# Graph attention on one core: the steps of the edge sums moved by one to three places in an eight-step order

## The chip, the cores and the metric

The program runs on one core of one Trainium2 chip. The metric is the device time of one execution in microseconds (us); lower is better. The core has a matrix engine (PE; its weight loads are shown apart as PEld), a vector engine (DVE), a scalar engine (ACT), GpSimd (POOL) and a queue engine that starts transfers (SP). Each works through its own list of instructions in the order in which the kernel was written out, and waits where an instruction needs another engine's result.

## What is computed

A graph of 12,500 nodes with 412,500 edges, sorted by target. Cut to what matters:

```
q, k, v, h = x @ Wq + bq, x @ Wk + bk, x @ Wv + bv, x @ Wn + bn
eh    = edge_features @ We + be
hmid  = leaky_relu(concat(q[src], k[tgt], eh) @ A1 + b1, 0.2)      # first layer, 128 wide
scores= leaky_relu(hmid @ A2 + b2, 0.2)                            # 8 heads
w     = softmax(scores.mean(-1), axis=0)                           # over all edges
out   = segment_sum(w[:, None] * v[tgt], src)                      # sums by source node
y     = layernorm(h + out) * gamma + beta
result= layernorm(x + y)
```

## The kernel before

Two streams of work are written into one order. The **edge stream** (`make`, lines 811 to 1081) takes the 403 groups of 1,024 edges in the given order. For each it multiplies one-hot matrices and edge features into "records" (`rows`, L940 and L947: the k and edge parts of the first layer beside v), evacuates them from the matrix engine's output banks (`evacuate`, L958 and L959, ACT) and scatters them by source block into a table `rtab` with POOL's indirect transfers (L970). Beside that DVE builds one-hots (L860 to L880) and the places of the records (L910 to L923), with counts on PE (L889). A group has six pieces.

The **sum stream** (`sums_of`, from line 1118) reads the records back by blocks of source nodes. There are 250 units of up to 16 tiles of 128 records, in ten rounds of 25. A unit goes through these functions:

- `load` starts the transfer of its records into `rt` (L1154, SP); `sources`, `turned`, `put` and `spread` bring the source numbers into `rowB`; `load_q` fetches `qs`.
- four times, for four tiles each: `onehot` (L1232, DVE), `hidden` (L1244 and L1254, PE: the first-layer rows), `copied` (L1265, ACT: out of the bank), `leaky` (L1269, DVE).
- once: `scores` (L1280, PE), `above` (function `above_zero`, L1294, ACT: the tile z), `heads` (L1306, PE), `maxima` (L1316 and L1321, DVE), `maximum` (L1327, PE), `reference` (L1336 and L1337, DVE), `weights` (L1346, ACT).
- four times: `select` (L1355, DVE, tile ohs), `weigh` (L1369, ACT, tile ohw), `add` (L1402, PE, into the bank psm).
- once: `lowered` (L1388 and L1391, ACT), `before_it` (L1379, SP: the table `old`), `total` (L1419, in the first rounds L1412, DVE: psm into old), `store` (L1431, SP).

The sum stream's order is a table of numbers, `lags` (line 1109): each function has a step, counted from the unit's own step s0, and a unit begins every 8 steps. So all functions of successive units share a frame of 8 steps. Within a step the older unit's work stands first; a few calls (`copied`, `leaky`, `maximum`) are put at the end of their step. While edge groups are left, the steps are spread evenly between the pieces of the edge groups, some 1.1 to 1.6 pieces to a step; what is left of the steps then runs alone, and a closing part normalizes the 98 blocks of nodes.

Buffers that bear on the order: psm is one bank (in the last round a second one is there, and units alternate), psS one, the ring of banks for rows, hidden and scores has five, ohs two, ohw three, hm six, rt six (eight in the last round).

Of the kernel before, what the change touches and what calls it, by code (L numbers as in the profile page):

```python
# [478 lines left out]
def sorted_path(  # L479
# [266 lines left out]
    above = const.tile([P, P], BF)  # L746
# [362 lines left out]
    def lags(p):  # L1109

        return dict(
            every=EVERY, lead=25 if p == NR - 1 else 19, sources=-13, turned=-12, spread=-7, q=-7,
            onehot=-2, copied=2, leaky=4, scores=12, above=14, heads=15, maxima=17, maximum=18,
            reference=20, weights=21, old=16, lowered=24, select=19, weigh=21,
            add=(24, 25, 27, 28), total=30, store=33,
        )

    def sums_of(bp):


        plans, s0, free, starts, ends = [], 19, ([], []), {}, {}
        for p, bs, t in units:
            nt = len(bs) * t
            nk = -(-nt // 4)
            o = lags(p)
            if plans:
                s0 += plans[-1][4]["every"]


            mine = free[spare_buffer(len(plans))]  # L1130
            held = MORE if mine is free[1] else BLKS
            load_at = mine[-held] + 1 if len(mine) >= held else 0
            s0 = max(s0, load_at + o["lead"] - 1)
            if plans:
                s0 = max(s0, plans[-1][2] + EVERY)
            if plans:
                s0 += (plans[0][2] - s0) % EVERY
            load_at = max(load_at, s0 - o["lead"])
            mine.append(s0 + o["add"][-1])
            starts.setdefault(p, load_at)  # L1140
            ends[p] = load_at
            plans.append((nt, nk, s0, load_at, o))
        steps = {}

        def do(step, fn, *args, late=0):
            steps.setdefault(max(int(step // 1), 0), []).append((late + step % 1, fn, args))
# [288 lines left out]
        def pieces(i):  # L1435
            at = list(range(0, plans[i][0], 4)) + [plans[i][0]]
            return list(zip(at[:-1], at[1:]))

        for i, (nt, nk, s0, load_at, o) in enumerate(plans):
            do(load_at, load, i)  # L1440
            do(s0 + o["sources"], sources, i)
            do(s0 + o["turned"], turned, i)
            do(s0 + o["turned"], put, i)
            do(s0 + o["spread"], spread, i)
            do(s0 + o["q"], load_q, i)
            for k, (c, c1) in enumerate(pieces(i)):
                n, s = c1 - c, s0 + 2 * k
                t = units[i][2]
                for u in range(-(-c // t), (c1 - 1) // t + 1):
                    do(s + o["onehot"], onehot, i, u)  # L1450
                do(s, hidden, i, c, c, n, k)
                do(s + o["copied"], copied, i, c, c, n, k, late=1)
                do(s + o["leaky"], leaky, i, c, c, n, k, late=1)
            do(s0 + o["scores"], scores, i, 0, nt)
            do(s0 + o["above"], above_zero, i)
            do(s0 + o["heads"], heads, i, 0, nt)
            do(s0 + o["maxima"], maxima, i)
            do(s0 + o["maximum"], maximum, i, late=1)
            do(s0 + o["reference"], reference, i)
            do(s0 + o["weights"], weights, i)  # L1460
            do(s0 + o["old"], before_it, i)
            do(s0 + o["lowered"], lowered, i)
            for j, t0 in enumerate(range(0, nt, 4)):
                n = min(4, nt - t0)
                if t0 % SEL == 0:
                    m = min(SEL, nt - t0)
                    do(s0 + o["select"] + 2 * j, select, i, t0, m)
                do(s0 + o["weigh"] + 2 * j, weigh, i, t0, n)
                do(s0 + o["add"][j], add, i, t0, n)
            do(s0 + o["total"], total, i)  # L1470
            do(s0 + o["store"], store, i)
# [350 lines left out]
    with tc.manual_schedule():  # L1822
# [9 lines left out]
        for i, _ in enumerate(_ for p in range(NP) for _ in make(p)):  # L1832
            while fills and fills[-1][0] <= i:
                fill_piece(*fills.pop()[1])
            while made < nt and made * n0 < i * nt:
                next(tabs, None)
                made += 1
            while sent < ne and sent * n0 < i * ne:
                next(more, None)
                sent += 1  # L1840
            if i == n1:
                for _ in tabs:
                    pass
                for _ in more:
                    pass
                spans()
                covered()
                tab_pool.close()
                steps, starts = sums_of(pool("blk", BLKS))
            if i < n1:  # L1850
                continue
            while r + 1 < NR and i >= 6 * begun[r + 1]:
                r += 1
            if r + 1 < NR:
                until = starts[r] + (starts[r + 1] - starts[r]) * (i - 6 * begun[r]) / (
                    6 * (begun[r + 1] - begun[r])
                )
                while done < until:
                    for fn, args in steps[done]:
                        fn(*args)  # L1860
                    done += 1
# [86 lines left out]
```

## Time and profile before

| what | value |
| --- | --- |
| runs shown | 5669.4, 5674.84, 5681.69 us; median 5674.84 us |
| the profiled execution's own time | 5666.23 us |
| its span from the first to the last instruction | 5664.4 us |
| mean granted PE clock over it | 0.831 |

The profile is of one execution. A group's row reads: line, engine, operation, the tile written and those read, shapes, how often; behind the bar the busy time in us and the mean of one in ns; behind the next bar the time that the engine sat idle just before such instructions, and what ended it. A row of waits gives who waited for whom, the total in us, how often, and the longest. A table of stretches gives for each stretch its length, then each engine's busy time (with the number of instructions), the granted PE clock as a share of full speed, the busy share of the transfer engines and the rate in GB/s. The ends of matrix instructions are modelled, so their busy time is approximate.

### The profile page before, as it was taken

The numbers are of one execution on the slowest core, as the hardware profiler recorded it, in microseconds if no ns is written. First come the engines' busy times: TensorE is split into PE (matmuls) and PEld (weight loads), VectorE is DVE, ScalarE is ACT, GpSimd is POOL, SyncE is SP. The second block draws the span as 40 slices with busy tenths as digits, with TensorE's granted clock in tenths as the row PEclk, the third lists the DMA queues.
The fourth block names the chain that finished last, engine by engine and source line by source line (L and its number), as shares of the span: only waits on it lengthen the run. The fifth ranks groups of instructions, "written<-read, shape, count | busy, mean of one in ns | idle before, by whom it ended". The sixth has DMA issues, their size and how long they took to land. (4 is left out here: it accounts for less than half of the span.)

```text
span 5664.4 us, 91119 instructions
## 1 busy us (share of the span) xinstructions
PE 4379.9 (77%) x29928; PEld 3200.3 (56%) x29928; DVE 3987.4 (70%) x8452; ACT 3097.1 (55%) x8846; POOL 3431.3 (61%) x3279
## 2 busy tenths in 40 slices
PE   4555536777788888888888888888887888887997
PEld 2333324555565666555566665666665565655777
DVE  7777736666667777766677767777776776766787
ACT  2432214444555666555566666666665665655786
POOL 4777666666666655566666666665556666666113
PEclk6666657788888889888888888888888998888999
DMA  6888756677788888877788878887887887878985
GB/s 194 264 260 263 250 197 223 224 240 229 247 267 272 268 268 278 261 263 257 268 269 279 294 264 282 284 278 263 275 266 270 280 285 265 271 262 274 345 314 188
DMA packets 727116, 1487.05 MB, mean 263 GB/s; under 512 B 157377, under 2 KB 326356, under 8 KB 724839
## 3 DMA queue, kind: packets, MB, share of 16 engines
q1 hardware_dynamic: 535538, 1055.66, 57.4%
q0 software_dynamic: 154752, 424.43, 20.6%
q10 hardware_dynamic: 36340, 1.05, 0.4%
q8 instruction: 237, 3.88, 0.3%
q14 instruction: 249, 2.03, 0.1%
HBM read 901.45 MB, written 579.32 MB: 261 GB/s over the span
## 5 line engine op out<-in xcount | busy, mean ns | idle before, releaser
L970 POOL DMA_INDIRECT rtab<-rec,idx x3224 | 3346.1, 1038 | 1896.5 <-issue 846.7
L958 ACT ACTIVATE rec<-bank 128x512 f32<-128x512 f32 x1612 | 881.0, 594 | 1265.8 <-remote 482.9
L1402 PE MATMUL psm<-rt,ohw 128*128 128x128 f32 x7448 | 1227.5, 310 | 158.3 <-issue 146.3
L1369 ACT ACTIVATE ohw<-ohs,w 128x128 f32<-128x128 bf16 x3724 | 1216.6, 403 | 37.3 <-DVE ohs L1355 24.1
L1402 PEld LDWEIGHTS psm<-rt,ohw 128*128 128x128 f32 x7448 | 1069.7, 216 | 243.5 <-issue 198.6
L1265 ACT ACTIVATE hm<-bank 128x512 f32<-128x512 f32 x932 | 550.0, 590 | 605.9 <-PE psm L1402 146.3
L947 PE MATMUL bank<-WeS,eat 64*128 64x128 f32 x6448 | 730.2, 333 | 109.2 <-issue 105.9
L940 PE MATMUL bank<-kvs,ohd 128*128 128x256 bf16 x3224 | 589.5, 303 | 259.8 <-ACT rec L958 116.9
L910 DVE TENSOR_TENSOR ats<-pc,oh 128x792 f32<-128x792 f32 x403 | 393.6, 977 | 560.4 <-remote 202.8
L1244 PE MATMUL bank<-ident,rt 128*128 128x128 f32 x3724 | 670.4, 303 | 68.9 <-issue 64.2
L947 PEld LDWEIGHTS bank<-WeS,eat 64*128 64x128 f32 x6448 | 530.6, 215 | 337.1 <-issue 331.9
L1232 DVE TENSOR_SCALAR ohT<-rowB,iotaP,power 128x512 bf16<-128x512 uint8 (+1 forms) x980 | 569.2, 584 | 160.2 <-remote 57.0
L1254 PE MATMUL bank<-ohT,qs 128*128 128x512 bf16 (+3 forms) x2156 | 628.5, 385 | 48.1 <-issue 39.3
L1244 PEld LDWEIGHTS bank<-ident,rt 128*128 128x128 f32 x3724 | 473.2, 155 | 334.0 <-issue 227.8
L1269 DVE SCALAR_TENSOR_TENSOR hm<-hm 128x512 f32<-128x512 f32 x932 | 637.5, 684 | 9.5 <-ACT hm L1265 6.8
L880 DVE TENSOR_SCALAR ohd<-dstb,node 128x1152 bf16<-128x1152 uint8 x404 | 566.1, 1401 | 40.0 <-remote 31.3
L940 PEld LDWEIGHTS <-ohd 128*128 128x128 bf16 x3224 | 335.1, 110 | 442.0 <-issue 345.5
L1306 PE MATMUL psS<-headsum,z 128*128 128x4 f32 (+2 forms) x2000 | 304.4, 274 | 165.2 <-ACT z L1294 155.6
L1306 PEld LDWEIGHTS psS<-headsum,z 128*128 128x128 f32 (+2 forms) x2000 | 297.8, 224 | 224.3 <-ACT z L1294 199.4
L1355 DVE TENSOR_TENSOR ohs<-iotaE,sl 128x512 bf16<-128x512 bf16 x932 | 394.0, 423 | 36.5 <-ACT ohw L1369 32.8
L1280 PE MATMUL bank<-hm,A2s 128*32 128x512 f32 x1864 | 377.7, 664 | 42.7 <-issue 32.7
L921 DVE TENSOR_REDUCE pos<-ats 128x8 f32<-128x792 f32 x403 | 390.3, 968 | 2.6
(199 smaller groups left out, 3683.9 us busy)
## 6 DMA issues: line engine op xcount, KB each, us to landing
rt<-rtab SPq DMA_DIRECT2D x192, 2056.0 KB
eat<-in_ea SPq DMA_DIRECT2D x201, 512.0 KB
rt<-rtab SPq DMA_DIRECT2D x48, 1542.0 KB
qs<-qtab SPq DMA_DIRECT2D x240, 256.0 KB
atab<-old SPq DMA_DIRECT2D x240, 256.0 KB
old<-atab SPq DMA_DIRECT2D x216, 256.0 KB
rtab<-rec,idx POOLq DMA_INDIRECT x3224
dstb<-dtab SPq DMA_DIRECT2D x201, 256.0 KB
```

Of the source, the lines that this page charges most:

```text
L880: nc.vector.tensor_scalar(to, row[:, cols], node, None, op0=ALU.is_equal)
L940: nc.tensor.matmul(pk[h][:, i, :], ohd[h * (GT // 2) + j + i], kvs, start=(i == 0), stop=False,)
L947: nc.tensor.matmul(pk[h][:, i, :D], eat[half, (j + i) * P : (j + i + 1) * P], WeS[half, :], start=False, stop=(i == 1),)
L958: nc.scalar.activation(rec[:, h, :, : 2 * D], pk[h], AF.Copy)
L970: one_tile = nc.gpsimd.indirect_dma_start(out=rtab[:, :], out_offset=bass.IndirectOffsetOnAxis(ap=idxs[g][:, t : t + 1], axis=0), in_=rec[ ...
L1232: nc.vector.tensor_scalar(st["oh"][u][:, : t * P].rearrange("p (t q e) -> p t q e", q=4, e=32), st["rowB"][:, : nt * P] .rearrange("p (q t ...
L1244: nc.tensor.matmul(ph[:, j * P : (j + 1) * P], st["rt"][:, t0 + j, :D], ident, is_transpose=True, start=(j == 0), stop=False,)
L1254: nc.tensor.matmul(ph[:, cols], st["qs"][:, u, s, :], st["oh"][u][:, (j0 - u * t) * P : (j1 - u * t) * P], start=False, stop=(s == 1 and j ...
L1269: nc.vector.scalar_tensor_tensor(hm, hm, SLOPE, hm, op0=ALU.mult, op1=ALU.max)
L1306: nc.tensor.matmul(st["psS"][:, 3 * P + t0 + j : 3 * P + t0 + j + (nv - 1) * sw + 1 : sw], z[: 32 * nv, j * P : (j + 1) * P], headsum[: 32 ...
L1369: nc.scalar.activation(ohw[:, j, :], ohs[:, :, t0 % SEL + j], AF.Copy, scale=st["w"][:, t0 + j : t0 + j + 1])
L1402: nc.tensor.matmul(st["psm"][:, u * P : (u + 1) * P], ohw[:, j, :], st["rt"][:, t0 + j, D : 2 * D], start=(k == 0), stop=(k == t - 1),)
```

## The change

Only the numbers in `lags` change, with the two lines that read `select` and `weigh`, which become lists.

```
-            onehot=-2, copied=2, leaky=4, scores=12, above=14, heads=15, maxima=17, maximum=18,
-            reference=20, weights=21, old=16, lowered=24, select=19, weigh=21,
-            add=(24, 25, 27, 28), total=30, store=33,
+            onehot=-2, copied=2, leaky=3, scores=10, above=12, heads=13, maxima=15, maximum=16,
+            reference=18, weights=19, old=14, lowered=22, select=(17, 19, 21, 23),
+            weigh=(19, 21, 23, 25), add=(21, 23, 25, 27), total=29, store=32,
...
-                    do(s0 + o["select"] + 2 * j, select, i, t0, m)
-                do(s0 + o["weigh"] + 2 * j, weigh, i, t0, n)
+                    do(s0 + o["select"][j], select, i, t0, m)
+                do(s0 + o["weigh"][j], weigh, i, t0, n)
```

The units' own steps s0, the steps of `load` and the steps at which rounds begin come out the same. In the frame of 8 steps (a unit's `hidden` stands at 0, 2, 4, 6) the functions stand so:

| function | before | after |
| --- | --- | --- |
| hidden; copied; onehot | 0 2 4 6; 2 4 6 0; 6 0 2 4 | the same |
| leaky | 4 6 0 2 | 3 5 7 1 |
| scores, above, heads | 4, 6, 7 | 2, 4, 5 |
| maxima, maximum, reference, weights | 1, 2, 4, 5 | 7, 0, 2, 3 |
| select | 3 5 7 1 | 1 3 5 7 |
| weigh | 5 7 1 3 | 3 5 7 1 |
| add | 0 1 3 4 | 5 7 1 3 |
| total; lowered; before_it; store | 6; 0; 0; 1 | 5; 6; 6; 0 |
| load (all but the last round); spread and load_q | 5; 1 | the same |

So `heads` shares its step with the first `add` of the unit before it, which needs the bank psm that `total` of a still older unit empties in that same step. How this stands in the engines' lists is shown at two places.

The matrix engine around the heads (L1306) of one unit in the sixth round; L947 are edge rows, L889 counts, L1244 and L1254 one piece of first-layer rows, L1402 an add. Before:

```order
L947 MATMUL bank<-WeS,eat 128x128 x4
L889 LDWEIGHTS rest
L889 MATMUL pc<-few,rest 128x99
L889 LDWEIGHTS rest
L889 MATMUL pc<-few,rest 128x99
L1244 MATMUL bank<-ident,rt 128x128 x4
L1254 LDWEIGHTS qs
L1254 MATMUL bank<-ohT,qs 128x512
L1254 LDWEIGHTS qs
L1254 MATMUL bank<-ohT,qs 128x512
L1306 MATMUL psS<-headsum,z 128x4 x4
```

The same unit's heads in the changed kernel:

```order
L947 MATMUL bank<-WeS,eat 128x128 x4
L1402 MATMUL psm<-rt,ohw 128x128 x4
L1244 MATMUL bank<-ident,rt 128x128 x4
L1254 LDWEIGHTS qs
L1254 MATMUL bank<-ohT,qs 128x512
L1254 LDWEIGHTS qs
L1254 MATMUL bank<-ohT,qs 128x512
L1402 MATMUL psm<-rt,ohw 128x128 x4
L1306 MATMUL psS<-headsum,z 128x4 x4
```

Before, a piece of first-layer rows stands right ahead of the heads. Now the first add of a unit stands there, and the last add of the unit before it stands one piece of first-layer rows earlier; between the two adds, on DVE, comes the total.

The vector engine around a total (L1419) of the same round; L1355 is a select, L1232 a one-hot, L1269 a leaky, L1201 and L1207 the sources, L921 and L923 places of records. Before:

```order
L1232 TENSOR_SCALAR ohT<-rowB,iotaP,power 128x512
L1269 SCALAR_TENSOR_TENSOR hm<-hm 128x512
L1355 TENSOR_TENSOR ohs<-iotaE,sl 128x512
L1419 SCALAR_TENSOR_TENSOR old<-old,by,psm 128x512
L1232 TENSOR_SCALAR ohT<-rowB,iotaP,power 128x512
L1269 SCALAR_TENSOR_TENSOR hm<-hm 128x512
L910 TENSOR_TENSOR ats<-pc,oh 128x792
```

The same unit's total in the changed kernel:

```order
L1355 TENSOR_TENSOR ohs<-iotaE,sl 128x512
L1201 SCALAR_TENSOR_TENSOR sl<-mask,rt 128x32
L1207 STREAM_TRANSPOSE slB<-sl 128x32
L1269 SCALAR_TENSOR_TENSOR hm<-hm 128x512
L1232 TENSOR_SCALAR ohT<-rowB,iotaP,power 128x512
L1419 SCALAR_TENSOR_TENSOR old<-old,by,psm 128x512
L1355 TENSOR_TENSOR ohs<-iotaE,sl 128x512
L1269 SCALAR_TENSOR_TENSOR hm<-hm 128x512
L1232 TENSOR_SCALAR ohT<-rowB,iotaP,power 128x512
```

Before, one-hot and leaky stand together and selects alone; now a leaky follows a select and a one-hot stands alone, and the total has moved ahead of the select.

## The prediction

> **What bounds the kernel now.** I read the page's first two parts, then a table of stretches, then the waits of the matrix engine inside the longest stretch.
>
> ```profile
> PE 4379.9 (77%) x29928; PEld 3200.3 (56%) x29928; DVE 3987.4 (70%) x8452; ACT 3097.1 (55%) x8846; POOL 3431.3 (61%) x3279
> ...
> PEclk6666657788888889888888888888888998888999
> ```
>
> The chain of waits at the end covers only the last normalization, so it says nothing of the middle. Averages hide stages; the stretches part them:
>
> ```profile
> 0.00:900.00 900.00, 444.20 (x2509) 297.85 (x2510) 624.80 (x1088) 265.71 (x517) 591.35 (x571) 0.67 0.76 240
> 900.00:1500.00 600.00, 459.10 (x2938) 325.48 (x2936) 372.74 (x754) 289.01 (x840) 394.92 (x385) 0.80 0.68 225
> 1500.00:5200.00 3700.00, 3075.20 (x21395) 2245.74 (x21393) 2648.85 (x5618) 2195.07 (x6441) 2330.78 (x2254) 0.86 0.81 272
> 5200.00:5500.00 300.00, 273.09 (x2067) 212.28 (x2067) 222.45 (x546) 238.55 (x729) 61.95 (x44) 0.96 0.93 341
> ```
>
> The columns of busy time are PE, PEld, DVE, ACT, POOL. Until 900 us there are no sums, so the change does not touch that. From 1500 to 5200 us both streams run: PE is busy 3075 of 3700 us (83%), DVE 72%, POOL 63%, ACT 59%. The matrix engine is nearest to its limit, and what can be won is some of its 625 us of idle time. From 5200 us the sums run alone at 91%. Who holds PE up in the long stretch:
>
> ```profile
> PE psS L1306 <- ACT z L1294: 130.5, 68, 6.8
> PE psm L1402 <- issue: 116.5, 204, 1.8
> ...
> PE bank L947 <- issue: 78.8, 137, 1.2
> ...
> PE bank L940 <- ACT rec L958: 41.9, 27, 5.9
> ...
> PE psm L1402 <- DVE old L1419: 3.1, 5, 1.2
> ```
>
> Two kinds of idle time are to be seen. The rows that end on "issue" wait for nothing that the trace knows, and no order of functions is known to shorten them. The largest real wait is that of the heads (L1306) for z, the scalar engine's product of the scores. The wait that could replace it, an add (L1402) for the total (L1419) that empties its bank, is 3.1 us today. Over the whole run the heads' wait is
>
> ```profile
> PE psS L1306 <- ACT z L1294: 155.6, 88, 7.7
> ```
>
> that is 88 of 250 units, 1.77 us each. A unit's length in the long stretch comes from the weights, one each:
>
> ```profile
> L1346 ACT ACTIVATE w<-S,ref 128x16 f32<-128x16 f32 (+2 forms) x195 | 59.4, 305 | 38.6 <-issue 19.5 <-DVE ref L1337 8.3 <-DVE ohd L880 6.6
> ```
>
> 195 units in 3700 us: 19.0 us a unit, 2.37 us a step.
>
> **The change part by part.** No instruction of work is added or removed; all costs are waits that come or go. The scale of PE's pieces is read from one place in the timeline where it runs without a break:
>
> ```profile
> 3631.33 1.06 PE L1306 MATMUL psS<-headsum,z 128*128 128x4 f32 x8 [0.74 <-ACT z L1294]
> 3632.25 1.14 PE L1402 MATMUL psm<-rt,ohw 128*128 128x128 f32 x8
> 3633.22 0.60 PE L1244 MATMUL bank<-ident,rt 128*128 128x128 f32 x4
> 3633.66 0.59 PE L1254 MATMUL bank<-ohT,qs 128*128 128x512 bf16 x2
> 3634.09 0.60 PE L940 MATMUL bank<-kvs,ohd 128*128 128x256 bf16 x4
> 3634.62 0.71 PE L947 MATMUL bank<-WeS,eat 64*128 64x128 f32 x8
> 3635.27 0.27 PE L889 MATMUL pc<-few,rest 128*128 128x99 bf16 x2
> 3635.37 1.12 PE L1402 MATMUL psm<-rt,ohw 128*128 128x128 f32 x8
> 3636.32 0.60 PE L1244 MATMUL bank<-ident,rt 128*128 128x128 f32 x4
> 3636.76 0.59 PE L1254 MATMUL bank<-ohT,qs 128*128 128x512 bf16 x2
> 3637.19 0.27 PE L1327 MATMUL psS<-ident,mx 128*128 128x128 f32 x1
> ```
>
> From start to start an add takes 0.97 us (3632.25 to 3633.22), a piece of first-layer rows 0.87 (3636.32 to 3637.19), a block of edge rows 1.18 (3634.09 to 3635.27). The first line shows the wait for z in the act: heads ready, 0.74 us lost.
>
> (a) **Scores to heads.** Scores, z and heads keep their distances (2 steps, then 1), with two pieces of first-layer rows between scores and heads before and after. New is the first add of the older unit right ahead of the heads: 0.97 us of work while ACT finishes z. Each of the 88 waits shrinks by at most that: 88 x 0.97 = 85 us; as some are shorter than 0.97 us I take 70. The bounds are nothing (z comes later by as much) and 155.6 us (all of it).
>
> (b) **Total to add.** Before, four steps lie between a unit's last add and the next unit's first, with the total in the middle. Now there are two, and the total stands in the same step as the first add. Its duration is known:
>
> ```profile
> L1419 DVE SCALAR_TENSOR_TENSOR old<-old,by,psm 128x512 f32<-128x512 f32 (+1 forms) x225 | 164.8, 732 | 165.0 <-remote 69.6 <-PE bank L947 30.4 <-PE bank L1254 18.8
> L880 DVE TENSOR_SCALAR ohd<-dstb,node 128x1152 bf16<-128x1152 uint8 x404 | 566.1, 1401 | 40.0 <-remote 31.3 <-PE pc L889 3.1 <-PE bank L1254 2.9
> ```
>
> Between the two adds PE has one piece of first-layer rows, 0.87 us, and in many units a block of edge rows, 1.18 more. The total's 0.73 us fits under that by 0.14 us, if DVE begins it as soon as the last add is done. The 165.0 us of idle time in front of totals say that DVE today often stands there waiting for PE; in other units it comes late, for instance behind the edge stream's one-hot of 1.40 us. The last round has a second bank, so 224 boundaries count. The bounds: nothing, and 224 x 0.73 = 164 us (every total exposed); where also a one-hot of 1.40 us stands ahead, more. I take 0.15 us each, 34 us, near the lower bound because the cover in the order exceeds the price. Behind a waiting add stand the heads, and behind those, on DVE and PE, the maxima two steps later and the maximum one more.
>
> [...]
>
> (c) **Leaky to scores.** A leaky now stands one step after its copy, not two, and the scores one step after the last leaky, not two. The rows:
>
> ```profile
> L1269 DVE SCALAR_TENSOR_TENSOR hm<-hm 128x512 f32<-128x512 f32 x932 | 637.5, 684 | 9.5 <-ACT hm L1265 6.8 <-ACT rec L959 0.9 <-issue 0.3
> L1280 PE MATMUL bank<-hm,A2s 128*32 128x512 f32 x1864 | 377.7, 664 | 42.7 <-issue 32.7 <-PE psm L1402 3.5 <-DVE oh L860 0.8
> ```
>
> Leakies wait 6.8 us in all for their copies and the scores not visibly for leakies. With a step of 2.37 us left, a copy and a leaky of 0.68 us still fit. Between nothing and 250 x 0.68 = 171 us (the last leaky wholly exposed) I take 10 us, near the row's present nothing.
>
> (d) **The load behind the last add.** `load` stays at its step, while the last add that frees its buffer stands one step earlier. On SP's queue this is the largest wait:
>
> ```profile
> SPq L1154 <- PE psm L1402: 415.7, 65, 13.5
> SPq L1154 <- remote: 342.7, 33, 16.3
> ```
>
> Other loads stand behind it on SP, those of rowB and qs three to four steps on. The engines feel little of it: DVE's one-hots wait for rowB
>
> ```profile
> DVE ohT L1232 <- DMA rowB<-row: 47.1, 24, 4.8
> ```
>
> Between nothing and 47 us I take 10 us of gain, nearer to nothing, since the records have further steps in hand.
>
> (e) The rest at nothing. Select to weigh, reference to weights, maxima to maximum keep their distances. Weigh to add becomes 2 steps throughout (3, 2, 2, 1 before); DVE's and ACT's moved instructions lie under PE, and if that cover goes, the wait appears in (a) to (c). The loads of `old` and the stores on SP move by two and one steps and keep their distance from the total's side. The closing part begins two steps sooner, under 2 x 2.37 = 5 us.
>
> **The sum**: -70 + 34 + 10 - 10 = -36 us. Against the profiled execution (5666.23 us: span 5664.4 and 1.8 around it) that is 5630 us. That execution lies 8.6 us under the median of the runs shown, so I add 8.6: **5639 us**, 0.6% faster.
>
> **The rivals.**
>
> *The bank psm becomes the loop* (slower). Place: the add ahead of the heads. Price: 164 us if each total is exposed, 75 of the 224 with a one-hot of 1.40 us ahead add 105; the heads' whole 156 us is then absorbed, so +113 us, 5788 us; with half of the lateness about 5735. It decides from a mean wait of 0.36 us a boundary (80 us of gains in (a) and (d) over 224). For it: DVE is busy 72% and does edge work in lumps, and the margin is 0.14 us. Against it: the 165 us in which DVE already waits in front of totals. Chance 0.36, with smaller mishaps of the same loop.
>
> *Nothing comes of it* (within 0.2%, 5664 to 5686 us). The idle time leaves the heads and appears on other lines: PE's waits for "issue" on L1402 and L947 (195 us in the long stretch) would grow by what the heads lose. For it: these waits are not tied to one line. Chance 0.16.
>
> *All of z's wait goes and the clock rises.* -156 us from (a), with nothing lost in (b): 5519 us. The long stretch runs at a granted 0.86; at 0.88 its 3075 us of PE work would need 70 us less, 5449 us. Chance 0.12. [...]
>
> **How the numbers follow.** The forecast's own case, 5590 to 5663 us, has 0.36. A measurement of this kernel tells about 0.2% from no change. Faster by more: 0.36 + 0.12 = 0.48; within: 0.16; slower: 0.36. As both signs hold much of the chance, the range goes from 5545 us (a good part of the third rival) to 5765 us (most of the first); the likeliest case's own range is 5590 to 5663.
>
> **What would show it.** Right: the heads' wait for z falls from 155.6 to about 85 us or less, the adds' wait for totals stays under 50 us, PE's share in 1500 to 5200 us rises over 83%. (c) is wrong if scores come to wait for leakies; (d) if SP's load waits as long as before. The forecast is wrong if adds wait for totals more than 80 us, or if "issue" grows by what z gives up.

## The result, and the profile after

The changed kernel is slower: 5749.43 us (median of 4 runs, 5732.72 to 5765.95) against 5672.12 us (4 runs), ratio 1.0128 with a 95% interval of 1.0107 to 1.0148. The forecast was 5639 us. Two more timings beside the kernel before gave 1.0095 (1.0073 to 1.0117) and 1.0112 (1.0090 to 1.0133). The profiled execution took 5749.56 us, its span is 5747.8 us, 83.4 more than before.

The page of the changed kernel: busy time by engine, PE in 40 slices, and the granted clock.

```profile
PE 4427.8 (77%) x29928; PEld 3269.4 (57%) x29928; DVE 4001.7 (70%) x8452; ACT 3098.6 (54%) x8846; POOL 3352.6 (58%) x3279
...
PEclk6676667777888889778888888888987888888999
```

The work is the same and busy shares hardly move. Of the 83.4 us, 47.9 are a longer busy time of PE (4427.8 against 4379.9 us, at a mean granted clock of 0.818 against 0.831) and 35.5 are idle time (span less busy time). Whether the waits below lower the clock is not shown. The table of stretches of the changed kernel (length; PE, PEld, DVE, ACT, POOL busy; clock, transfers' share, GB/s):

```profile
1500.00:5200.00 3700.00, 3032.54 (x21054) 2254.13 (x21053) 2614.77 (x5533) 2158.18 (x6330) 2236.16 (x2218) 0.85 0.81 268
5200.00:5500.00 300.00, 265.50 (x1854) 198.41 (x1852) 207.59 (x481) 210.91 (x637) 89.32 (x78) 0.91 0.88 308
```

In the same 3700 us of the long stretch PE gets through 21,054 products instead of 21,395, 82% busy instead of 83%. Its waits in the changed kernel (who waits, for whom: total us, times, longest):

```profile
PE psm L1402 <- DVE old L1419: 182.0, 72, 6.3
PE psm L1402 <- issue: 148.0, 234, 3.1
...
PE psm L1402 <- DVE old L1412: 32.3, 13, 6.1
```

The heads' wait for z, 155.6 us before, no longer appears among the waits. In its place adds (L1402) wait for totals: 214.3 us in 85 waits, 2.5 us each, or 0.96 us over each of 224 boundaries, where the forecast had 0.15. PE's idle time ahead of adds, first before, then after, grew by 291 us in all:

```profile
L1402 PE MATMUL psm<-rt,ohw 128*128 128x128 f32 x7448 | 1227.5, 310 | 158.3 <-issue 146.3 <-ACT ohw L1369 3.8 <-DVE old L1419 3.1
```
```profile
L1402 PE MATMUL psm<-rt,ohw 128*128 128x128 f32 x7448 | 1261.2, 316 | 449.4 <-DVE old L1419 182.0 <-issue 148.0 <-DVE old L1412 32.3
```

Some 70 us of that are waits that ACT ended, the tile ohw among them. Idle time ahead of the heads and of edge rows fell, so that 35.5 us are left. The groups of DVE that belong to it, in the changed kernel (busy and mean, then idle time ahead):

```profile
L1419 DVE SCALAR_TENSOR_TENSOR old<-old,by,psm 128x512 f32<-128x512 f32 (+1 forms) x225 | 165.0, 734 | 265.0 <-remote 145.9 <-PE psm L1402 56.8 <-PE bank L1254 27.6
L1269 DVE SCALAR_TENSOR_TENSOR hm<-hm 128x512 f32<-128x512 f32 x932 | 630.6, 677 | 197.2 <-ACT hm L1265 130.8 <-issue 40.1 <-ACT rec L959 14.1
```

The total lasts 0.73 us as before, but DVE stands idle ahead of it for 265.0 us (165.0 before). So totals are not late because DVE is busy; DVE is there and waits. One place of the changed kernel's timeline shows this (start, length, engine, line; idle time and its end in brackets):

```profile
2923.81 1.06 PE L1280 MATMUL bank<-hm,A2s 128*32 128x512 f32 x8
...
2925.73 1.05 PE L1402 MATMUL psm<-rt,ohw 128*128 128x128 f32 x8
...
2928.35 0.59 PE L1254 MATMUL bank<-ohT,qs 128*128 128x512 bf16 x2
...
2930.00 0.54 DVE L1232 TENSOR_SCALAR ohT<-rowB,iotaP,power 128x512 bf16<-128x512 uint8 x1
...
2934.03 0.75 DVE L1419 SCALAR_TENSOR_TENSOR old<-old,by,psm 128x512 f32<-128x512 f32 x1 [3.49 <-remote]
2934.13 1.08 ACT L958 ACTIVATE rec<-bank 128x512 f32<-128x512 f32 x2 [2.61 <-remote]
...
2934.92 2.05 PE L1402 MATMUL psm<-rt,ohw 128*128 128x128 f32 x8 [5.97 <-DVE old L1419]
...
2936.76 1.71 PE L1306 MATMUL psS<-headsum,z 128*128 128x4 f32 x8
```

The unit's last add ends by its record at 2926.78, and PE does edge rows, counts and one more piece of first-layer rows. DVE is free from 2930.54. Yet the total begins at 2934.03, 7.25 us after the add's recorded end. The row says "remote", since no instruction's recorded end lies near the signal that released it. But the trace tells whose signal it was: the total waits for a semaphore that only matrix-engine instructions raise, and it was raised at 2934.00. So it is PE's own signal that comes late, and not the transfer of `old` or another engine. Over the whole run, 309.6 of the 309.9 us in which DVE stands idle ahead of totals end on this semaphore. ACT, which waits on the same one for edge rows, is released 0.10 us after DVE. PE is idle for 5.97 us, then the add follows the total by 0.14 us, and the heads, whose z ended at 2927.74 on ACT, come behind the add at 2936.76. Here the signal comes 7.22 us after the recorded end.

The last round, in which psm has two banks, is slower too. The scores' products there (180 in each kernel, 5310 to 5528 us before, 5372 to 5610 after), first before, then after, by the groups of that stretch:

```profile
L1280 PE MATMUL bank<-hm,A2s 128*32 128x512 f32 x180 | 24.5, 605 | 0.0
```
```profile
L1280 PE MATMUL bank<-hm,A2s 128*32 128x512 f32 x180 | 36.7, 620 | 0.0
```

and one unit of it in the changed kernel's timeline:

```profile
5436.98 1.89 PE L1280 MATMUL bank<-hm,A2s 128*32 128x512 f32 x8
5437.08 0.68 DVE L1269 SCALAR_TENSOR_TENSOR hm<-hm 128x512 f32<-128x512 f32 x1
5437.82 0.14 PEld L1280 LDWEIGHTS bank<-hm,A2s 128*32 128x32 f32 x2 [0.69 <-DVE hm L1269]
```

The scores begin before the last leaky and stop in the middle for it: 1.89 us a unit where the kernel before takes 1.07 (the median of units in that round). From the start of the 226th weights (L1346) to that of the 250th the round takes 242 us, 224 before.

### The profile page after: what moved, and what is told of

It reads as the page before. It is cut to its first block, busy times and chain, and to the rows that moved or that the text cites. A ratio compares the mean times of both kernels' runs of the same rounds, so it can differ in the third digit from the quotient of the medians.

```text
span 5747.8 us, 91233 instructions
## 1 busy us (share of the span) xinstructions
PE 4427.8 (77%) x29928; PEld 3269.4 (57%) x29928; DVE 4001.7 (70%) x8452; ACT 3098.6 (54%) x8846; POOL 3352.6 (58%) x3279
## 5 line engine op out<-in xcount | busy, mean ns | idle before, releaser
L970 POOL DMA_INDIRECT rtab<-rec,idx x3224 | 3267.6, 1014 | 2036.3 <-issue 841.0
L1402 PE MATMUL psm<-rt,ohw 128*128 128x128 f32 x7448 | 1261.2, 316 | 449.4 <-DVE old L1419 182.0
L1402 PEld LDWEIGHTS psm<-rt,ohw 128*128 128x128 f32 x7448 | 1115.9, 222 | 614.8 <-issue 272.7
L1269 DVE SCALAR_TENSOR_TENSOR hm<-hm 128x512 f32<-128x512 f32 x932 | 630.6, 677 | 197.2 <-ACT hm L1265 130.8
L947 PE MATMUL bank<-WeS,eat 64*128 64x128 f32 x6448 | 725.3, 342 | 54.7 <-issue 52.8
L940 PE MATMUL bank<-kvs,ohd 128*128 128x256 bf16 x3224 | 607.7, 313 | 197.2 <-ACT rec L958 92.6
L1244 PE MATMUL bank<-ident,rt 128*128 128x128 f32 x3724 | 691.2, 309 | 79.6 <-issue 75.6
L1254 PE MATMUL bank<-ohT,qs 128*128 128x512 bf16 (+3 forms) x2156 | 642.3, 390 | 65.3 <-issue 42.9
L947 PEld LDWEIGHTS bank<-WeS,eat 64*128 64x128 f32 x6448 | 533.0, 223 | 277.8 <-issue 274.6
L1244 PEld LDWEIGHTS bank<-ident,rt 128*128 128x128 f32 x3724 | 473.6, 159 | 345.7 <-issue 238.8
L1232 DVE TENSOR_SCALAR ohT<-rowB,iotaP,power 128x512 bf16<-128x512 uint8 (+1 forms) x980 | 563.8, 579 | 64.8 <-DMA rowB<-row 48.2
L940 PEld LDWEIGHTS <-ohd 128*128 128x128 bf16 x3224 | 352.0, 115 | 358.5 <-issue 267.4
L1355 DVE TENSOR_TENSOR ohs<-iotaE,sl 128x512 bf16<-128x512 bf16 x932 | 391.4, 420 | 23.5 <-ACT ohw L1369 17.9
L921 DVE TENSOR_REDUCE pos<-ats 128x8 f32<-128x792 f32 x403 | 391.1, 970 | 2.8
L1280 PE MATMUL bank<-hm,A2s 128*32 128x512 f32 x1864 | 341.2, 645 | 17.4 <-issue 10.5
L1419 DVE SCALAR_TENSOR_TENSOR old<-old,by,psm 128x512 f32<-128x512 f32 (+1 forms) x225 | 165.0, 734 | 265.0 <-remote 145.9
L1306 PEld LDWEIGHTS psS<-headsum,z 128*128 128x128 f32 (+2 forms) x2000 | 325.9, 245 | 11.8 <-issue 9.7
```

Source lines behind the costliest of these rows:

```text
L940: nc.tensor.matmul(pk[h][:, i, :], ohd[h * (GT // 2) + j + i], kvs, start=(i == 0), stop=False,)
L947: nc.tensor.matmul(pk[h][:, i, :D], eat[half, (j + i) * P : (j + i + 1) * P], WeS[half, :], start=False, stop=(i == 1),)
L970: one_tile = nc.gpsimd.indirect_dma_start(out=rtab[:, :], out_offset=bass.IndirectOffsetOnAxis(ap=idxs[g][:, t : t + 1], axis=0), in_=rec[ ...
L1232: nc.vector.tensor_scalar(st["oh"][u][:, : t * P].rearrange("p (t q e) -> p t q e", q=4, e=32), st["rowB"][:, : nt * P] .rearrange("p (q t ...
L1244: nc.tensor.matmul(ph[:, j * P : (j + 1) * P], st["rt"][:, t0 + j, :D], ident, is_transpose=True, start=(j == 0), stop=False,)
L1254: nc.tensor.matmul(ph[:, cols], st["qs"][:, u, s, :], st["oh"][u][:, (j0 - u * t) * P : (j1 - u * t) * P], start=False, stop=(s == 1 and j ...
```

## The experiments

All change the table `lags` alone, but for one that moves a bank. They ran in five groups, each on a chip of its own; each ratio is to the kernel before on the same chip: 5761.12 us for e1 to e4, 4891.82 for e5 to e8, 5675.86 for e9 to e12, 4886.60 for e13 to e16, 5678.54 for e17 and e18.

| runs | kernel | ratio (95% interval) |
| --- | --- | --- |
| e1 | changed, total one step sooner | 1.0127 (1.0099 to 1.0154) |
| e2; e10 | leaky one step, all from scores on two steps sooner, distances of before | 1.0081 (1.0057 to 1.0106); 1.0076 (1.0053 to 1.0098) |
| e3 | leaky alone | 1.0018 (0.9999 to 1.0036) |
| e4; e11 | spacing of adds and total alone | 1.0102 (1.0078 to 1.0125); 1.0097 (1.0066 to 1.0128) |
| e5; e14 | before with two banks psm | 1.0013 (1.0003 to 1.0023); 1.0008 (0.9993 to 1.0024) |
| e6; e15 | changed with two banks psm | 0.9971 (0.9961 to 0.9980); 0.9970 (0.9960 to 0.9980) |
| e8; e12 | front half of the shift alone | 0.9922 (0.9909 to 0.9935); 1.0002 (0.9986 to 1.0019) |
| e16 | the same, leaky one more step sooner | 0.9963 (0.9950 to 0.9976) |
| e7, e13; e18 | e2 with leaky one more step sooner | 1.0001 (0.9992 to 1.0010), 1.0001 (0.9990 to 1.0013); 1.0072 (1.0052 to 1.0092) |
| e9; e17 | changed | 1.0095 (1.0073 to 1.0117); 1.0112 (1.0090 to 1.0133) |

**Can the total come sooner? (e1)** Against the changed kernel:

```
-            add=(21, 23, 25, 27), total=29, store=32,
+            add=(21, 23, 25, 27), total=28, store=32,
```

> The changed kernel with the total one step earlier (28 in place of 29), so that DVE's list has it one step ahead of the next unit's first add. Theory loop-late (the add waits because DVE comes late to the total): about half of the loss goes, ratio to the kernel before 1.004 to 1.008, and the adds' wait for totals falls from 214 to about 100 us. Theory loop-completion (the total itself cannot begin sooner, because the last add's result is reported some us after its modelled end): no gain, ratio 1.011 to 1.015, DVE's idle time before totals grows from 265 us to over 350. Theory elsewhere (the loss comes from the scores or from the order of z and heads): ratio unchanged at 1.013 and the adds' wait unchanged.

No gain over the changed kernel's 1.0095 to 1.0128 on other chips; on this chip that kernel was not timed. The total's group and the adds' waits in e1:

```profile
L1419 DVE SCALAR_TENSOR_TENSOR old<-old,by,psm 128x512 f32<-128x512 f32 (+1 forms) x225 | 165.2, 734 | 463.8 <-remote 243.9 <-PE psm L1402 97.5 <-PE bank L1254 51.7
```
```profile
PE psm L1402 <- DVE old L1419: 159.2, 66, 7.3
...
PE psm L1402 <- DVE old L1412: 29.1, 7, 7.5
```

DVE stands ahead of the total for 463.8 us instead of 265.0, and adds wait 188.3 us in place of 214.3. What is late is the release of the total, not its place on DVE, as the second theory had it.

**The spacing of adds and total alone (e4, e11).** Against the kernel before:

```
-            add=(24, 25, 27, 28), total=30, store=33,
+            add=(23, 25, 27, 29), total=31, store=34,
```

> The kernel before with only the adds, total and store moved: adds at 23, 25, 27, 29, total 31, store 34, so that in the frame the total and the next unit's first add share a step, just ahead of the heads, as in the changed kernel; scores, z, heads and leaky stay. Theory loop: the loss of the mixed stretch appears here too, ratio 1.008 to 1.013, with 150 to 250 us of adds waiting for totals and the heads' wait for z under 20 us. Theory chain or leaky: ratio 0.997 to 1.003.

> The spacing of adds and total alone, on the chain of before (1.010 on the chip of the first four; the psm loop without the shift). Theory 1, the loop is a loop on every chip: 1.006 to 1.012. If the loop only bites where completions come late: under 1.004 on a chip under 5000 us.

About 1.0% slower, twice. The waits in e11:

```profile
PE psm L1402 <- DVE old L1419: 197.8, 83, 7.7
...
PE psm L1402 <- issue: 158.5, 221, 6.7
...
PE psm L1402 <- DVE old L1412: 35.0, 12, 8.2
```

Without any shift of the chain, adds wait 232.8 us for totals, and no wait of the heads for z is left. So the spacing of adds and total by itself makes a loss of the size that the change has. In e11 it is nearly all idle time of PE: 50 us more than before, with 9 us more of busy time.

**The shift without that loop (e2, e10).** Against the changed kernel:

```
-            add=(21, 23, 25, 27), total=29, store=32,
+            add=(22, 23, 25, 26), total=28, store=31,
```

> The chain from leaky to total two steps sooner as in the changed kernel, but the adds and the total spaced as in the kernel before (22, 23, 25, 26; total 28; store 31), so that two steps lie between a total and the next unit's first add. Theory loop (one bank psm): the adds' wait for totals falls under 30 us and the ratio to the kernel before is 1.000 to 1.005, of which up to 0.003 is the last leaky exposed to the scores in the last round. Theory chain (the shifted scores, z and heads cost it): ratio stays 1.010 to 1.015 though the adds' wait is gone.

> The shift of two steps without the psm loop again (1.008 on the chip of the first four). Order alone: 1.006 to 1.010. Chip-dependent: as before on a chip over 5600 us, 0.990 to 1.003 on one under 5000 us.

Still 0.8% slower, between the two cases expected. The waits in e10:

```profile
PE psS L1306 <- ACT z L1294: 118.8, 68, 4.9
...
PE psm L1402 <- DVE old L1419: 6.4, 7, 1.6
```

Adds no longer wait, the heads wait for z again, somewhat less than before (118.8 against 155.6 us), and time is lost all the same. It is no idle time of the matrix engine. The busy times in e10 and in e18 (below, the same shift with an earlier leaky):

```profile
PE 4425.1 (78%) x29928; PEld 3232.0 (57%) x29928; DVE 4005.4 (70%) x8452; ACT 3093.0 (54%) x8846; POOL 3379.9 (59%) x3279
```
```profile
PE 4427.4 (78%) x29928; PEld 3224.4 (56%) x29928; DVE 3996.6 (70%) x8452; ACT 3097.4 (54%) x8846; POOL 3383.0 (59%) x3279
```

For the same 29,928 products PE is busy 45 and 48 us longer than before, while its idle time is 1275.2 and 1284.1 us against 1284.5. The granted clock is no lower (0.830 and 0.833 against 0.831), and the ends of products are modelled; why they take longer stays open. This was not in the prediction at all.

**Leaky alone (e3).** Against the kernel before:

```
-            onehot=-2, copied=2, leaky=4, scores=12, above=14, heads=15, maxima=17, maximum=18,
+            onehot=-2, copied=2, leaky=3, scores=12, above=14, heads=15, maxima=17, maximum=18,
```

> The kernel before with only the leaky one step sooner (3 in place of 4). Theory loop: 0.998 to 1.002, no part of the loss. Theory leaky (DVE stalls on copies that ACT has not yet made, and passes that on): 1.004 to 1.010, with over 100 us of DVE's idle time before leakies as in the changed kernel (197 us).

1.0018, at the edge of what can be told from no change. DVE's idle time ahead of leakies rises from 9.5 to 346.7 us, for some 10 us of time, 21 at most by the interval: DVE's waits there cost next to nothing.

**The front half of the shift alone (e8, e12).** Against the kernel before; selects, weighs, adds, total and store stay:

```
-            onehot=-2, copied=2, leaky=4, scores=12, above=14, heads=15, maxima=17, maximum=18,
-            reference=20, weights=21, old=16, lowered=24, select=19, weigh=21,
+            onehot=-2, copied=2, leaky=3, scores=10, above=12, heads=13, maxima=15, maximum=16,
+            reference=18, weights=19, old=16, lowered=24, select=19, weigh=21,
```

> Only the front half of the shift: leaky one step and scores, above, heads, maxima, maximum, reference and weights two steps sooner; selects, weighs, adds, total and store stay where they were before. If the front half costs (scores close behind the leaky, or z's place): 1.006 to 1.010, as the whole shift. If the back half costs (selects, weighs and adds against first-layer rows): 1.000 to 1.003, as leaky alone. Adds' wait for totals stays under 10 us.

> The front half of the shift again (0.992 where the kernel before took 4892 us). On a chip under 5000 us: 0.990 to 0.994. On one over 5600 us: 1.003 to 1.010 if the front half is what costs in e2_shift, 0.998 to 1.003 if the back half is.

e12 is the clearest run of the study. The group of the heads, and two waits, in e12:

```profile
L1306 PE MATMUL psS<-headsum,z 128*128 128x4 f32 (+2 forms) x2000 | 290.2, 264 | 43.8 <-issue 40.0 <-ACT z L1294 3.3
```
```profile
PE psm L1402 <- issue: 199.5, 322, 1.7
...
PE psm L1402 <- DVE old L1419: 13.1, 15, 2.1
```

The wait for z has gone from 155.6 to 3.3 us, adds wait 13.1 us, and the time is that of before, 1.0002. The idle time is now ahead of other lines: PE's waits for "issue" on adds rise from 146.3 to 199.5 us and on heads from 8.2 to 40.0. Taking the heads' wait away is worth nothing here: PE's idle time falls by 21 us in all, and its busy time grows by 25 (4405.3 us). On the chip of e8 the same kernel gains 0.8%, the most of the four that ran there.

**Is it the tight place between leaky and scores? (e7, e13, e18, e16)** e2, and for e16 the front half, with one more number changed:

```
-            onehot=-2, copied=2, leaky=3, scores=10, above=12, heads=13, maxima=15, maximum=16,
+            onehot=-2, copied=2, leaky=2, scores=10, above=12, heads=13, maxima=15, maximum=16,
```

> The shift of two steps without the psm loop (as e2_shift, which was 1.008 of before), with each leaky one more step sooner, so that two steps lie again between the last leaky and the scores. Theory S (the scores stand too close behind the last leaky): back to 1.000 to 1.004. Theory P (what costs is where the chain stands against the first-layer and edge rows): 1.007 to 1.010 as e2_shift. The vector engine's idle time in front of leakies rises further over the 431 us of e2_shift in either case.

> The shift of two steps without the psm loop, with each leaky one more step sooner, so that two steps lie again between the last leaky and the scores (1.0001 where the kernel before took 4892 us; the shift with tight scores was 1.0076 to 1.0081 where it took 5676 and 5761 us). On a chip over 5600 us: theory tight (the tight place from last leaky to scores makes the chain late, and only where two steps of slack follow, as in the front half alone, is that absorbed): 0.999 to 1.003. Theory place (where selects, weighs, adds and total stand against first-layer and edge rows): 1.006 to 1.010.

> The shift of two steps without the psm loop and with two steps between last leaky and scores. Where the kernel before takes under 5000 us: 0.999 to 1.002, as twice before. Where it takes over 5600 us (not timed there so far): theory tight 0.999 to 1.003, theory place 1.006 to 1.010.

> The front half of the shift alone, with the leaky one more step sooner (two steps from last leaky to scores, two more steps from weights to weighs). On a chip over 5600 us: 0.997 to 1.001, since the last round no longer loses its 6 us to scores behind the leaky; heads' wait for z stays under 20 us. On a chip under 5000 us: 0.988 to 0.994.

e7 and e13 ran where the kernel before takes under 4900 us, and there the shift costs nothing with free scores; the tight form of it was not timed there. e18 decides on the other kind of chip: 1.0072 with two steps between last leaky and scores, as with one. The theory of the tight place falls for the mixed rounds. e16, on another chip of e8's kind, stands 0.4% above e8's ratio and above what was expected, so the earlier leaky probably has a price there. It frees the scores of the last round (1.06 us a unit in the median, 1.50 in e8), but the round is no shorter: 232 against 229 us.

What the shift moves beside that shows on SP's queue. The wait of the load of rowB (L1222) for its source, in the kernel before, in e12, in e10 and in e18:

```profile
SPq L1222 <- DMA row<-slT: 34.1, 15, 5.2
```
```profile
SPq L1222 <- DMA row<-slT: 63.8, 22, 6.7
```
```profile
SPq L1222 <- DMA row<-slT: 388.7, 96, 9.6
```
```profile
SPq L1222 <- DMA row<-slT: 414.4, 96, 9.6
```

It is long just in the two kernels in which the back half moved with the front, and other loads stand behind it on SP. In the changed kernel it is 113.4 us. That this is the cause of the 0.8% was not tried, and more speaks against it. DVE's wait for rowB is 19.7 us in e10 and 17.2 in e18, less than the 47.1 before. And in e13, where the shift costs nothing, the same wait on SP is the longest of all:

```profile
SPq L1222 <- DMA row<-slT: 1037.4, 219, 9.3
```

**Two banks for psm (e5, e6, e14, e15).** In both kernels:

```
-    RING = 5
+    RING = 4
...
-    psmp = pool("psm", 1, space=PSUM)
+    psmp = pool("psm", 2, space=PSUM)
```

> The kernel before with the row ring one bank shorter (4) and the freed bank given to psm, which then has two in every round: an add no longer has to wait for the total of the unit just before. Theory 1 (the psm loop is the whole loss): this is near before, within 1%, a little slower for the shorter ring; its partner e6 then stands within 0.4% of it. Theory 2 (the chain standing two steps earlier costs by itself): the partner e6 stays 0.7 to 1.3% slower than this run.

> The changed kernel with two banks for psm and a ring of 4. Both theories: adds' wait for totals (182 + 32 us in the changed kernel) falls under 20 us. Theory 1: ratio to e5 1.000 to 1.004. Theory 2: ratio to e5 1.007 to 1.013, near the 1.008 that the shift without the psm loop cost.

> The kernel before with a ring of 4 banks and two for psm, as the partner of the next run: 1.000 to 1.006 on any chip (1.0013 where the kernel before took 4892 us).

> The changed kernel with a ring of 4 and two banks for psm (0.9958 of its partner where the kernel before took 4892 us). On a chip over 5600 us: if the psm loop is all that the changed order loses, 0.996 to 1.003 of its partner; if the tight scores or the place of the back half lose too, 1.005 to 1.010 of its partner, and adds wait for totals under 20 us either way.

Both pairs ran on chips on which the kernel before takes under 4900 us. With a second bank the changed order is 0.4% faster than its partner (4875.74 against 4898.88, 4870.77 against 4890.25 us), and adds wait for no totals. Neither case of the expectation of e6 had that gain. Its last round still takes 241 us against 227 (e15, e14): 14 us lost there. As the profiled span is 21.6 us shorter (4861.7 against 4883.3) and 5 us more are lost behind the round, some 40 are gained ahead of it. Whether the second bank repairs the loss on a chip like that of the prediction did not come to be tried.

**The changed kernel again (e9, e17).** The kernel is as it was; both runs fell on chips where the kernel before takes some 5677 us.

> The changed kernel itself, timed once more, since the last four kernels ran on a chip on which the kernel before takes 4892 us, and the changed kernel has not been timed there. If its loss is one of the order alone: 1.011 to 1.015 wherever it runs. If the loss needs a chip that reports the matrix engine's completions late (where engines wait long for issue): 1.010 to 1.015 where the kernel before takes over 5600 us, 0.995 to 1.006 where it takes under 5000 us.

> The changed kernel once more, to see its ratio on the chip of this call. Where the kernel before takes under 5000 us (not timed there so far; with two banks the changed order was 0.996 of its partner): the loop on the bank psm costs on any chip, then 1.004 to 1.012; or it bites only where the engines wait for issue, then 0.994 to 1.002, and adds' wait for totals is under 100 us. Where the kernel before takes over 5600 us: 1.008 to 1.014, as twice before.

The loss stands, at 1.0% and 1.1%. On a chip under 5000 us the changed kernel with one bank was not timed.

## Why the prediction was wrong

By its own points: the heads' wait was to fall to 85 us or less, and it vanished. The adds' wait for totals was to stay under 50, and was named wrong from 80; it came to 214.3. PE's share in the long stretch was to rise over 83%, and fell to 82%.

**(b) Total to add: the step that failed.** It took 0.15 us for each of 224 boundaries, "near the lower bound because the cover in the order exceeds the price", with the condition "if DVE begins it as soon as the last add is done". The cover was counted from the recorded end of the last add. The total is released later than that. Where DVE already stands waiting, totals of the changed kernel begin a median of 3.7 us after the recorded end in the rounds ahead of the last (97 totals; 3.0 and 3.9 us in the profiles of e9 and e17). In the last round, without edge work, a typical total follows its add by 0.04 us. e1 shows that an earlier total only waits longer. The 165.0 us of idle time ahead of totals, which the prediction took as a sign that DVE is there in time, were this same lateness: in the trace of the kernel before, totals for which DVE waits begin a median of 4.4 us after the recorded end (71 totals). It could have been read there. The order then had four steps, 9.5 us, to hide it; two are not enough. Measured alone, in e11 and e4, the new spacing costs 0.97% and 1.02%, 55 and 59 us, where the term said 34 with bounds of 0 to 164. What that spacing would cost with a prompt signal, no run shows.

**(a) Scores to heads.** The direction was right: all of z's wait went, not 70 us. The cover was counted too small. Not one add but, in most units, two now stand between scores and heads, since the unit before also has its last add there (step 3, between 2 and 5); the timeline above shows scores at 2923.81, adds at 2925.73 and 2934.92, then the heads. Before, there is none, and in e10, where there is none again, the wait is back. The value was wrong too: each us of it was counted as a us of time, and e12, on another chip of the same kind, shows 152 us of that wait gone for nothing (1.0002, that is 1 us, interval -8 to +11). This is the rival "Nothing comes of it", with the idle time on "issue", as far as this term goes. With (a) at nothing and (b) at 55, the prediction's own sum would be 55 + 10 - 10 = +55 us, 5730 us by its own base: the sign right, and a good part of the 77 us measured.

**(c) Leaky to scores.** 10 us were taken. In the mixed rounds leaky alone costs 1.0018, and e18 shows no price of the tight place. In the last round scores last 36.7 in place of 24.5 us, but that is hardly what lengthens it: e12 with slow scores (1.85 us a unit) takes 230 us and e18 with free ones (1.07) 229, against 224 before. The shift alone adds 5 to 6 us there (e10 too, 230), the spacing alone none (e11, 224), and the two together 17 to 19 (after, e9, e17). Why together is open.

**(d) The load behind the last add.** SP's wait for adds fell about as thought:

```profile
SPq L1154 <- PE psm L1402: 221.4, 45, 10.7
```

from 415.7 us, but nothing came of it: DVE's wait for rowB stayed,

```profile
DVE ohT L1232 <- DMA rowB<-row: 48.2, 20, 6.0
```

47.1 us before.

**(e) The rest at nothing** missed the shift itself, 0.76% and 0.81% in e10 and e2 with the distances on the chain as before (leaky apart). With the back half left in place (e12) nothing is lost. The losses don't add: spacing and shift alone would make 1.7 to 1.8%, together they are 0.95 to 1.28%.

The rival *The bank psm becomes the loop* named the mechanism and the place, and its case with half of the lateness (5735 us) lies nearest to the result, though that figure halves the 113 us; by the rival's own netting, half of the lateness (135 us) less 156 would be no loss. And it put the lateness on a busy DVE behind one-hots; it lay in PE's signal to the total. Its netting of the adds' waits against the heads' would fit here (214.3 us after, 155.6 + 3.1 before, so 56 more), yet it fails in e12 (16.4 us of the two together, 142 less, no change) and in e10 (125.2, 34 less, and 43 us slower). The third rival, *All of z's wait goes and the clock rises*, had the first half right; the clock in the long stretch went from 0.86 to 0.85. No run shows its term of 70 us for a clock of 0.88, which was the author's estimate: in e12, with 3.3 us left of z's wait, that stretch keeps 0.86 and PE is busy 3077.2 us of it, against 3075.2 before. What stays open: why the back half's place costs 0.8% of longer busy time, and why PE's signal comes late.

## What to carry to other kernels

A bank that is emptied and refilled in one loop needs cover for the whole way there and back, and the matrix engine's part of that way (a median of 3.7 us in the changed kernel, 0.04 us in e14 and e15) is read from when others were released by it, not from where its record ends: measure from the last product's end to the start of its reader, in the units in which the reader was already waiting. The trace of the kernel before held that number, 4.4 us, against a cover counted to tenths of a us. A wait in the list of waits is a bound on a gain and no forecast of it: e12 removed the largest one of the busiest engine, 152 us, without moving the time (1.0002). Where parts of an order can be moved apart, time them apart, since neither their waits nor their losses added up here.

## What the runs showed of the hardware

The same kernel took 5672 to 5761 us on some chips and 4887 to 4892 on others, 16 to 18% apart, with the same instructions. Each chip served one group of runs, so whether the chip itself makes this or something else about its group is not shown. Of the 781 us between the spans of the kernel before and of e14 (the same order, one bank moved), 466 are PE's busy time, at a granted clock of 0.831 and 0.886, and 315 its idle time. On the slower ones the trace has waits that end on "remote" or "issue": PE waits 146.3 us for "issue" on adds in the kernel before. In e14, on a faster chip, no such row is among PE's waits, and transfers are busy 97% where the kernel before had 81%:

```profile
1500.00:4400.00 2900.00, 2524.56 (x20224) 1922.56 (x20225) 2492.24 (x5317) 2057.54 (x6088) 2210.65 (x2126) 0.94 0.97 328
```

On the faster chips the signal to totals is prompt, with edge work beside it: where DVE waits for a total, it begins a median of 0.04 us after the add's recorded end (17 totals in e14, 23 in e15, ahead of the last round), and in these two no row ends on "remote" (in e5 the largest such row is 10.2 us). The totals' group in e15:

```profile
L1419 DVE SCALAR_TENSOR_TENSOR old<-old,by,psm 128x512 f32<-128x512 f32 (+1 forms) x225 | 164.7, 732 | 43.9 <-PE psm L1402 43.5
```

So the lateness that decided (b) was seen on the slower chips alone, and one order is worth different things on the two kinds: the front half alone gains 0.8% on one (e8) and nothing on the other (e12), the shift with free scores loses nothing on one (e13) and 0.7% on the other (e18). What makes the waits and the late signals on the slower chips was not found.
